# End of attention in a post-norm attention and mixture-of-experts kernel: routing of sequence five at double pace, scatters of sequence six around the last scale, second biases summed ahead of the expert blocks

## The chip, the cores and the metric

The kernel runs on one core of a Trainium2 chip. The metric is the device time of one execution in microseconds. Times of single instructions come from one profiled execution, counted from the start of its span.

## What is computed

Eight sequences of 512 tokens with 128 features go through one layer of causal attention (16 heads of 8) and one layer of experts (14 experts, each token goes to its two best), each with a residual and a normalisation after it:

```python
x = layernorm(x + attention(x))              # Q, K, V, softmax, output projection, biases
probs = softmax(x @ gate_w.T)
top2_p, top2_i = top_k(probs, 2)
w = top2_p / maximum(top2_p.sum(-1), 1e-10)
hh = gelu(einsum('nd,edf->nef', x, w1) + b1)
all_out = einsum('nef,efd->ned', hh, w2) + b2
moe = w[:, 0:1] * all_out[n, top2_i[:, 0]] + w[:, 1:2] * all_out[n, top2_i[:, 1]]
x = layernorm(x + clip(x + moe, -100, 100))
```

The expert outputs are added up with weights, and so are the second biases: for a token this part is the sum of its two weights times the `b2` rows of its two experts. The kernel computes it apart from the experts, as one small matrix product of the weights laid out by expert (`w_all`) with `b2`.

## The kernel before

**Three stages.** Attention first, for all sequences; then the expert blocks; then the sums and the last normalisation. Tokens lie on the 128 partitions, four tiles (`NQ`) to a sequence. Sequences are numbered from zero, so six is the last but one and seven the last.

**Attention runs in steps.** There are 32 units (eight sequences, four groups of four heads) of five steps each. In step `s` the kernel emits the front of step `s` (scores and row maxima), the back of step `s - 12` (scores again, shifted by the maximum, then exponentials on ScalarE and causal selects on GpSimd), and after them whatever has been entered for that step in the table `jobs`. Fronts end at step 159, the last back is at step 171. Each engine takes its instructions in the order in which they are emitted, so a place in `jobs` is a place in the queues of all engines. No planner reorders anything. Jobs of one step run in the order in which they were entered; a job that enters itself again for the next step therefore comes after those that were there from the beginning.

**Jobs around the end.** `product` multiplies the exponentials with the values five and six steps after the back of its unit began, `evacuate` copies the result, `divide`, `project` and `residual` (for the last sequence; others go by way of DRAM with `divisors`, `invert`, `multiply`) give attention plus residual in `y_sb` and its statistics on VectorE. Two steps after `residual`, `route(b)` starts. It is a generator: `proceed` runs it up to its next `yield` once a step, or twice a step for sequence six, its pace. Its pieces are: scale and shift of the normalisation on GpSimd (`layernorm_scale`), normalising on ScalarE, transposes and logits on TensorE, the two best experts on VectorE, a count of the tokens before each one on TensorE, target rows `to_i` on VectorE, two GpSimd operations that fill `w_all`, and then eight indirect DMAs issued from GpSimd, the scatters, one to a piece, which put the token rows into `XS`, sorted by expert.

**The drain.** After the last step `fill` pads the experts' regions in `XS` by DMAs from SP and ScalarE, and VectorE works out which expert each block of 256 rows belongs to. The first block's load waits for all of these writes.

**Expert blocks.** There are 45. `load` brings rows and weights, `turn` transposes (two TensorE transposes and a copy on VectorE), `expert_in` multiplies with the first weights and applies GELU on ScalarE, `expert_out` multiplies with the second weights, scales by the routing weight on VectorE (`ob`) and scatters two tiles to `OS` from GpSimd. `load` runs four blocks ahead, `turn` two, `expert_in` one. After every fourth `expert_out` (blocks 2, 6, 10 and so on) `biases(c)` treats one sequence: a TensorE transpose of `w_all`, a copy on VectorE, a product with `b2_blk` on TensorE, and an addition on VectorE of that product and `y_sb` into a buffer `acc` of its own:

```python
            if i >= 0:
                expert_out(i)
                if i % 4 == 2 and i // 4 < B:
                    biases(i // 4)
```

**The end.** `gather` reads `OS` back, `add_up` sums `acc` and the two gathered parts on TensorE, `residual_2` and `store` clip, add, normalise and write. The result is collected in `z_sb`, which is the region of the input `x_sb`.

## Time and profile before

| | us |
|---|---|
| Median of three runs (643.71 to 650.58) | 649.47 |
| The profiled execution, its own time | 656.64 |
| Its span | 654.9 |
| Last front's maximum begins | 391.34 |
| Copy of the last attention product (`oT`) | 417.57 |
| Last statistics of sequence seven end | 426.45 |
| Rows of the first expert block are loaded from | 456.63 |
| First and last scatter of the expert blocks | 469.02 and 611.63 |

| Engine | busy us | share of the span |
|---|---|---|
| TensorE matmuls | 506.3 | 77% |
| TensorE weight loads (beside the matmuls) | 305.2 | 47% |
| VectorE | 378.4 | 58% |
| GpSimd | 334.6 | 51% |
| ScalarE | 281.7 | 43% |

In rows of groups, of a tile or of an order in time, an instruction stands with its line (L503), its engine (PE is TensorE, PEld its weight loads, DVE VectorE, ACT ScalarE, POOL GpSimd, SP the engine that only issues DMAs), and its output and inputs by the program's names. Groups end with busy time and mean duration in ns, and then the idle time ahead of them and who ended it. Rows in order of time begin with the start and the duration in us. Rows of stretches have the length, then the busy time of PE, PEld, DVE, ACT and POOL with counts, the granted TensorE clock, the DMA share and GB/s. The forty digits of a busy row are tenths of 16.4 us slices.

### The profile page before, as it was taken

To read this page: it belongs to the slowest core of one execution; us is meant where nothing else is said; L and a number is where in the kernel's file an instruction comes from. 1 tells how busy PE (TensorE), PEld (TensorE's weight loads), DVE (VectorE), ACT (ScalarE), POOL (GpSimd) and SP (SyncE) were. 2 spreads that over 40 slices of the span, in tenths; PEclk is the share of its full clock that TensorE was granted. 3 is DMA by queue.
4 is the path that set the end of the run, shared out by engine and by line. 5 is a ranking of instruction groups with operands and counts; after the bars stand their busy time and mean duration, and the time that the engine had idled before them with its cause. 6 is when DMAs were issued, how large, how long until landed. Compare 5 with 4: busy or idle time off the path is not lost.

```text
span 654.9 us, 11179 instructions
## 1 busy us (share of the span) xinstructions
PE 506.3 (77%) x3458; PEld 305.2 (47%) x3458; DVE 378.4 (58%) x835; ACT 281.7 (43%) x437; POOL 334.6 (51%) x690
## 2 busy tenths in 40 slices
PE   2388989899889899799889898620788778777392
PEld 1145545445445455355355354310567667666140
DVE  4267677868848758758668674423344434443185
ACT  0213666666566566466466567210222222232034
POOL 5002333435664664664565767854255646566343
PEclk9865999989879879879699799655788988899696
DMA  5243434444354354253253020114664645553382
GB/s 157 73 146 99 115 99 155 134 139 141 109 163 133 103 162 141 98 173 124 67 162 120 34 71 27 45 44 156 176 170 141 165 138 155 144 152 107 99 206 82
DMA packets 79894, 80.63 MB, mean 123 GB/s; under 512 B 15820, under 2 KB 62005, under 8 KB 79834
## 3 DMA queue, kind: packets, MB, share of 16 engines
q1 hardware_dynamic: 68272, 67.89, 35.5%
q0 software_dynamic: 4928, 8.48, 3.9%
q10 hardware_dynamic: 6634, 3.55, 2.1%
q8 instruction: 27, 0.44, 0.3%
q14 instruction: 33, 0.27, 0.1%
HBM read 51.01 MB, written 31.66 MB: 126 GB/s over the span
## 4 chain that ended last, share of the span: by engine, by line
PE 54%; DVE 14%; ACT 9%; issue 8%; DMA 6%; SPq 4%; POOL 3%; ACTq 1%; another core or an unknown queue 1%; DVEq 0%; POOLq 0%
PE av L503 12%; PE f L360 10%; PE b L446 7%; PE h L940 6%; PE o L956 6%; ACT pt L481 5%; PE f L370 4%; DVE bn L196 2%; DVE mx L400 2%; PE bp L983 2%; DVE stats L197 2%; PE x L926 2%; ACT oT L513 2%; DVE mx L412 1%; DVE ob L964 1%
## 5 line engine op out<-in xcount | busy, mean ns | idle before, releaser
L481 ACT ACTIVATE pt<-b 128x1024 f32<-128x1024 f32 x160 | 162.4, 1023 | 49.6 <-PE b L446 44.7
L457 POOL TENSOR_SCALAR_AFFINE_SELECT pt<-pt 128x256 f32<-128x256 f32 (+1 forms) x224 | 96.2, 444 | 133.6 <-ACT pt L481 132.3
L360 PE MATMUL f<-kr,qr 72*128 72x384 bf16 (+3 forms) x512 | 123.8, 326 | 33.9 <-ACT pt L481 18.3
L220 POOL DMA_INDIRECT OS<-ob,bto_i x90 | 87.6, 974 | 74.1 <-DVE ob L964 36.6
L412 DVE TENSOR_REDUCE mx<-f 128x2 f32<-128x1024 f32 x64 | 78.2, 1224 | 60.5 <-PE f L370 43.7
L446 PE MATMUL b<-qr,kr 75*128 75x384 bf16 (+3 forms) x512 | 102.5, 315 | 6.8 <-DVE mx L400 4.5
L503 PE MATMUL av<-pt,v_aug 128*32 128x512 f32 (+3 forms) x1024 | 96.6, 495 | 3.5 <-POOL pt L457 3.5
L370 PE MATMUL f<-causal_bf,ident_bf 128*128 128x256 bf16 (+1 forms) x320 | 87.1, 272 | 0.0
L360 PEld LDWEIGHTS <-qr 72*128 72x128 bf16 x512 | 53.4, 105 | 71.1 <-issue 49.7
L405 DVE TENSOR_REDUCE mx<-f 128x8 f32<-128x1024 f32 x64 | 77.7, 1222 | 12.8 <-PE f L370 10.9
L945 ACT ACTIVATE hT<-h,wt 128x256 f32<-128x256 f32 x90 | 37.5, 471 | 103.9 <-issue 101.2
L964 DVE TENSOR_SCALAR ob<-o,bxb 128x128 f32<-128x128 f32 x90 | 27.3, 346 | 67.5 <-PE o L956 28.4
L446 PEld LDWEIGHTS <-kr 75*128 75x128 bf16 x512 | 42.8, 101 | 38.6 <-issue 25.7
L956 PE MATMUL o<-wt,hT 128*128 128x128 f32 x360 | 52.9, 293 | 6.2 <-ACT hT L945 2.9
L940 PE MATMUL h<-bxT,wt 128*128 128x256 f32 x180 | 53.7, 427 | 4.9 <-DVE bxT L928 4.7
L503 PEld LDWEIGHTS av<-pt,v_aug 128*32 128x32 f32 x1024 | 29.2, 118 | 59.9 <-issue 43.4
L956 PEld LDWEIGHTS o<-wt,hT 128*128 128x128 f32 x360 | 51.6, 207 | 11.8 <-ACT hT L945 6.6
L400 DVE TENSOR_REDUCE mx<-f 128x4 f32<-128x1024 f32 x32 | 39.1, 1222 | 16.6 <-PE f L370 10.2
L370 PEld LDWEIGHTS <-ident_bf 128*128 128x128 bf16 x320 | 33.8, 106 | 18.9 <-issue 7.8
L220 POOL DMA_INDIRECT XS<-y_sb,to_i x32 | 32.5, 1015 | 13.4 <-issue 7.1
L940 PEld LDWEIGHTS h<-bxT,wt 128*128 128x128 f32 x180 | 34.6, 214 | 9.8 <-DVE bxT L928 5.6
L220 POOL DMA_INDIRECT XS<-second,to_i x32 | 32.2, 1007 | 8.2 <-issue 8.2
(170 smaller groups left out, 583.3 us busy)
## 6 DMA issues: line engine op xcount, KB each, us to landing
wt<-WP SPq DMA_DIRECT2D x45, 257.0 KB
kr<-ksc SPq DMA_DIRECT2D x32, 288.0 KB
qr<-qsc SPq DMA_DIRECT2D x96, 96.0 KB
osc<-oT SPq DMA_DIRECT2D x28, 256.0 KB
bxb<-XS SPq DMA_DIRECT2D x45, 130.0 KB
WP<-in_L_ffn_w_dram SPq DMA_DIRECT2D x28, 128.0 KB
qsc<-qpc SPq DMA_DIRECT2D x24, 128.0 KB
ksc<-kpc SPq DMA_DIRECT2D x24, 128.0 KB
```

Source lines behind the costliest of these rows:

```text
L220: inst = nc.gpsimd.indirect_dma_start(dst, bass.IndirectOffsetOnAxis(ap=idx, axis=0), src, None, bounds_check=bound, oob_is_err=False,)
L360: nc.tensor.matmul(ps[:, col : col + W], qr[u % RING][0:KR, j, qb * P : (qb + 1) * P], kr[u % RING][0:KR, j, :W], start=first, stop=False, ...
L370: nc.tensor.matmul(out, ident_bf, causal_bf[:, 0:n, :], start=False, stop=True, skip_group_check=True,)
L400: nc.vector.reduce_max(mx[:, :, 5], ps.rearrange("p b (s k) -> p (b s) k", s=2), axis=AX.X)
L405: nc.vector.reduce_max(mx[:, j : j + 2, 1:5], ps.rearrange("p b (s k) -> p b s k", k=P), axis=AX.X,)
L412: nc.vector.reduce_max(mx[:, j : j + 2, 7], ps, axis=AX.X)
L446: nc.tensor.matmul(ps[:, col : col + W], kr[u % RING][:, j, kb * P : (kb + 1) * P], qr[u % RING][:, j, kb * P :], start=first, stop=True, ...
L457: nc.gpsimd.affine_select(out=view, in_=view, pattern=[[0, k] for k in n] + [[1, P]], compare_op=ALU.is_ge, fill=0.0, base=0, channel_mult ...
L481: nc.scalar.activation(pt, ps, AF.Exp, scale=SCALE)
L503: nc.tensor.matmul(avs[u][HS * j : HS * (j + 1), kb * P :], v_aug[b % 2][:, kb, g * GH + j, :], p, start=(kb == 0), stop=(kb == 2),)
L940: nc.tensor.matmul(hp[:, f, :], wt[:, f * P : (f + 1) * P], xT, start=True, stop=True)
L956: nc.tensor.matmul(op[:, s, :], hT[:, f, s * P : (s + 1) * P], wt[:, F + f * D : F + (f + 1) * D], start=(f == 0), stop=(f == NFC - 1),)
```

## The change

Five things are changed.

- `biases` moves from the expert stage to the attention stage. It takes its PSUM tile from the caller (in attention one of the three `unit` tiles that backs use), its copy of the weights goes into the buffer of `recT`, and its result into `acc`, which is now the region of `x_sb`. Sequences zero to six are entered as jobs 4, 6, 8, 10, 11, 18 and 20 steps after the last front (step 159); sequence seven stays in the expert stage, at block 2.
- `route(5)` runs at two pieces a step, as `route(6)` did already.
- In the routing of sequence seven, two of the four normalisings go to VectorE.
- `w_all` is filled by a function `weigh`, called after the last scatter, and for sequence six after the first one; for sequence six two more empty pieces stand ahead of the scatters.
- In the expert stage the transposes `x` take a whole PSUM bank each, the biases have one buffer of two banks, and the last sums take the buffers of `x`.

```diff
+    acc = x_sb
+    weighed = set()
+    def biases(c, ps, pool):
+        assert c in weighed
+        ts = slice(c * NQ, (c + 1) * NQ)
+        nc.tensor.transpose(
+            ps[:, 0, 0:P],
+            w_all[:, ts, :].rearrange("p t s -> p (t s)"),
+            ident,
+        )
+        wT = pool.tile([P, T], FP, tag="recT", name=f"wT_{c}", bufs=1)[:, 0:P]
+        nc.vector.tensor_copy(wT, ps[:, 0, 0:P])
+        nc.tensor.matmul(
+            ps[:, 1, :], wT, b2_blk.rearrange("p t d -> p (t d)"), start=True, stop=True
+        )
+        nc.vector.tensor_tensor(
+            acc[:, ts, :],
+            ps[:, 1, :].rearrange("p (t d) -> p t d", d=D),
+            y_sb[:, ts, 0:D],
+            ALU.add,
+        )
...
                 t = b * NQ + i
+                if b == B - 1 and i % 2 == 1:
+                    nc.vector.tensor_scalar(
+                        y_sb[:, t, 0:D],
+                        y_sb[:, t, 0:D],
+                        rstd[:, i : i + 1],
+                        shift[:, i : i + 1],
+                        ALU.mult,
+                        ALU.add,
+                    )
+                    continue
                 nc.scalar.activation(
...
-            wide = rt("wide", [2, NQ, E])
-            nc.gpsimd.tensor_tensor(
-                wide, hot, w.unsqueeze(3).to_broadcast([P, 2, NQ, E]), ALU.mult
-            )
-            nc.gpsimd.tensor_tensor(w_all[:, ts, 0:E], wide[:, 0], wide[:, 1], ALU.add)
-            yield
+            def weigh():
+                weighed.add(b)
+                wide = rt("wide", [2, NQ, E])
+                nc.gpsimd.tensor_tensor(
+                    wide, hot, w.unsqueeze(3).to_broadcast([P, 2, NQ, E]), ALU.mult
+                )
+                nc.gpsimd.tensor_tensor(
+                    w_all[:, ts, 0:E], wide[:, 0], wide[:, 1], ALU.add
+                )
+            for _ in range(3 if b == B - 2 else 1):
+                yield
             for i in range(NQ):
                 for k, src in enumerate((y_sb[:, b * NQ + i, :], second[:, i, :])):
                     scatter("XS", XS[:, :], to_i[:, k, i : i + 1], src, E * CAP - 1)
+                    if b == B - 2 and i == 0 and k == 0:
+                        weigh()
                     yield
+            if b != B - 2:
+                weigh()
...
-                at(r + 2, proceed, r + 2, route(b), 2 if b == B - 2 else 1)
+                at(r + 2, proceed, r + 2, route(b), 2 if b in (B - 3, B - 2) else 1)
+        last_front = step_of(NU - 1, UN - 1)
+        for c, n in enumerate((4, 6, 8, 10, 11, 18, 20)):
+            at(last_front + n, lambda c: biases(c, unit(f"b2_{c}"), work), c)
...
-        name="ps_b", bufs=2, space=bass.MemoryType.PSUM
+        name="ps_b", bufs=1, space=bass.MemoryType.PSUM
...
-            tp = ps_x.tile([P, BT], FP, tag="x", name=f"x_{i}")
+            tp = ps_x.tile([P, T], FP, tag="x", name=f"x_{i}")[:, 0:BT]
...
-                if i % 4 == 2 and i // 4 < B:
-                    biases(i // 4)
+                if i == 2:
+                    biases(B - 1, ps_b.tile([P, 2, T], FP, tag="b2", name="b2_ps", bufs=1), ffn)
...
-            sums[c] = ps_b.tile([P, NQ, D], FP, tag="b", name=f"sum_{c}")
+            sums[c] = ps_x.tile([P, NQ, D], FP, tag="x", name=f"sum_{c}")
```

More of the change, by code (lines that the diff above doesn't have):

```diff
@@ L967, in expert_out @@
                 scatter("OS", OS[:, :], to_i[:, s : s + 1], ob[:, s, :], 2 * N - 1)
-        acc = ffn.tile([P, NT, D], FP, tag="acc", name="acc", bufs=1)
-        def biases(c):
-            ts = slice(c * NQ, (c + 1) * NQ)
-            wp = ps_b.tile([P, T], FP, tag="b", name=f"wp_{c}")
-            nc.tensor.transpose(
-                wp[:, 0:P],
-                w_all[:, ts, :].rearrange("p t s -> p (t s)"),
-                ident,
-            )
-            wT = ffn.tile([P, P], FP, tag="wT", name=f"wT_{c}")
-            nc.vector.tensor_copy(wT, wp[:, 0:P])
-            bp = ps_b.tile([P, T], FP, tag="b", name=f"bp_{c}")
-            nc.tensor.matmul(
-                bp, wT, b2_blk.rearrange("p t d -> p (t d)"), start=True, stop=True
-            )
-            nc.vector.tensor_tensor(
-                acc[:, ts, :],
-                bp.rearrange("p (t d) -> p t d", d=D),
-                y_sb[:, ts, 0:D],
-                ALU.add,
-            )
         AHEAD = 4
```

## The prediction, made before the result was known

> **What bounds the kernel now.** I read the page first, then tables by stretch, the chain in order of time, and the order of single instructions at the two places that the change touches. The profiled execution took 656.64 us, 654.9 of them span; the median of the runs shown is 649.47, so sums made in the trace are carried over to the median as differences.
>
> ```profile
> PE   2388989899889899799889898620788778777392
> PEclk9865999989879879879699799655788988899696
> L220 POOL DMA_INDIRECT OS<-ob,bto_i x90 | 87.6, 974 | 74.1 <-DVE ob L964 36.6
> L503 PE MATMUL av<-pt,v_aug 128*32 128x512 f32 (+3 forms) x1024 | 96.6, 495 | 3.5 <-POOL pt L457 3.5
> ```
>
> The busy rows show three stages: attention bound by TensorE up to about 400 us, a hole around 410 to 459 us (the drain: last backs, routing of the last two sequences, block plan), and the expert blocks to about 612 us. The change moves work from the third stage into the second, so both are to be priced. The stretches, with TensorE's busy time first and its granted clock near the end:
>
> ```profile
> 391.34:412.90 21.56, 18.50 (x154) 8.92 (x152) 10.37 (x36) 15.48 (x22) 16.97 (x39) 1.00 0.13 40
> 412.90:458.94 46.04, 12.84 (x60) 7.62 (x60) 15.68 (x72) 3.82 (x9) 28.02 (x45) 0.50 0.26 81
> 479.62:572.45 92.83, 73.77 (x414) 62.39 (x414) 39.18 (x155) 23.30 (x56) 54.53 (x57) 0.91 0.55 153
> 578.83:606.52 27.69, 19.52 (x122) 16.61 (x122) 10.70 (x46) 7.60 (x19) 17.52 (x18) 1.00 0.42 117
> ```
>
> 391.34 is where the last front ends. For 21.6 us after it TensorE is still 86% busy; the hole opens only later. In the drain the set of waits that counts is this one, GpSimd's:
>
> ```profile
> 425.77 0.97 POOL L220 DMA_INDIRECT XS<-y_sb,to_i  x1 [0.31 <-issue]
> 426.27 0.18 DVE L197 BATCH_NORM_AGGREGATE stats<-bn 128x2 f32<-128x6 f32 x1
> 427.04 0.98 POOL L220 DMA_INDIRECT XS<-second,to_i  x1 [0.30 <-issue]
> 428.33 0.97 POOL L220 DMA_INDIRECT XS<-y_sb,to_i  x1 [0.30 <-issue]
> 429.37 0.20 POOL L204 TENSOR_SCALAR rstd<-stats 128x4 f32<-128x4 f32 x1
> 431.30 1.65 ACT L645 ACTIVATE y_sb<-y_sb,shift,rstd 128x128 f32<-128x128 f32 x4 [9.50 <-POOL shift L207]
> ```
>
> The last statistics are there at 426.45, the scale starts at 429.37: 2.9 us behind sequence six's scatters. In the expert stage the biases and the scatters:
>
> ```profile
> L983 PE MATMUL bp<-b_blk,wT x16: 592/697/1061, 474.2 to 569.2; 128*128 128x512 f32 x16
> L986 DVE TENSOR_TENSOR acc<-bp,y_sb x8: 691/691/692, 476.1 to 569.8; 128x512 f32<-128x512 f32 x8
> PE bp L983 <- DVE wT L981: 13.8, 6, 3.3
> ...
> 578.83 0.97 POOL L220 DMA_INDIRECT OS<-ob,bto_i  x1 [1.57 <-DVE ob L964]
> ...
> 588.08 0.97 POOL L220 DMA_INDIRECT OS<-ob,bto_i  x1 [1.89 <-DVE ob L964]
> ...
> 597.32 0.97 POOL L220 DMA_INDIRECT OS<-ob,bto_i  x1 [1.87 <-DVE ob L964]
> ...
> 606.52 0.97 POOL L220 DMA_INDIRECT OS<-ob,bto_i  x1 [1.84 <-DVE ob L964]
> ```
>
> TensorE stands still at six of the eight biases, 13.8 us in all, for a copy that VectorE makes late. But the last four rows come after the last bias: even without biases GpSimd issues six scatters 1.28 us apart (three blocks), waits 1.9 us, and so on, 9.24 us a turn.
>
> **What the Trainium skill says.** "TensorE: Matmul & The Clock Gate", section "What's actually happening": the array falls to half clock after an idle window of about 3.4 us and needs as long a busy one to come back. The trace agrees: clock 1.00 until 412.9, then 0.50, and a bias matmul takes 592 to 1061 ns. "Perfetto Trace Analysis", section "Tensor Engine Instruction": a matmul's end is estimated, and the other engines' queues are strict FIFO. Both are seen here: the eviction of block 13 starts at 511.62 though its matmuls are drawn as over at 509.2, and ScalarE's normalising of sequence six stood behind the scale. So I count by starts of evictions and scatters, not by drawn matmuls.
>
> **The change part by part.**
>
> *Seven biases leave the expert blocks* (the one at the third block stays). Two readings. By scatters: blocks 3 to 31 span 479.62 to 572.45, 92.83 us for 28 blocks, 3.31 a block; the bias-free turns give 27.69 us for 9 blocks, 3.08. 28 x 0.238 = 6.7 us. By TensorE: the output matmuls of blocks 31 and 43 start at 570.73 and 603.87, 2.76 a block, and 28 x 0.55 = 15.5 us. The stage ends with the last scatter, at 612.6, so I stay near the first and take **8.5 us gained**; ends 3 (the middle bias cycle of four blocks, 12.72 us, against 12.31, seven times) and 15.5. Late next: GpSimd's scatters, 2.56 us a block at least.
>
> *Five biases (sequences zero to four) in the last back steps, 163 to 170.* Each is a transpose (0.27), a round trip to VectorE (copy 0.28, handed on in some 0.1 each way) and two matmuls at full clock (0.86 start to start): 1.6 us of TensorE, in order, 8.0 in all. The second stands behind residual of sequence six on VectorE: in the trace of before that row of work runs 399.05 to 401.93 while TensorE would be at the bias from about 400.2, so 1.8 us more of standing still, with backs, exponentials and the products of sequence seven queued behind. Against it: TensorE has 4.6 us of gaps between 391.34 and 417.5 (4.1 of them waits on selects that stand behind sequence five's scatters, or on ScalarE), which the biases fill, and the products at 414.6 run at half clock, 1.5 us more than before 412.9. Sum: 8.0 + 1.8 - 4.1 - 1.5 = +4.2 us at the last evacuation (417.57 now). The evictions with y (0.69 each) lie on VectorE, 52% idle there.
>
> *Sequence five at double pace.* It takes eight scatters (10.2 us of GpSimd) out of 403 to 418.8, where selects waited on them; that gain is in the 4.1 above. They now come two a step in steps 155 to 159: 10.2 + seven selects x 0.44 + maximum pieces 0.9 = 14.2 us on GpSimd in five steps of 2.1 us = 10.5. It falls 3.7 us behind; a product follows its selects by two steps (4.2 us), so it is nearly hidden. Its copy to `second` enters SP's queue at step 149, seven steps ahead of the scatter that reads it: nothing. VectorE's wait for the weights' reciprocal now falls into a step with a front. Cost taken +1, ends 0 and 4 (cover gone, and the clock with it).
>
> *Sequence six's scatters around the last scale.* From the last evacuation to the last statistics it is 8.88 us now; with a clock still full for transposes and projection I take 8.0: statistics at 417.57 + 5.2 + 8.0 = 430.8 against 426.45. Three scatters and the two weighing operations (0.37 and 0.34) stand ahead of the scale instead of five and two; begun at about 423 to 424.5 they are done by then. The 2.9 us queue goes; the scale starts at 430.8 against 429.37, **+1.4**. The five scatters behind it need 6.4 us and the next GpSimd work of routing comes some 9 us later: nothing.
>
> *Half of the last normalising on VectorE.* ScalarE's four take 1.65; two would save 0.8. But the biases of sequences five and six are ahead in VectorE's queue, each waiting for TensorE: copy 0.28, matmuls 1.1 (1.9 at half clock), eviction 0.69, twice, then two normalisings of 0.28: the last is ready 4.9 to 6.7 us after the statistics, where it is 3.6 us after the scale's start now. Net **+1.6**, ends 0.5 and 2.8.
>
> *Weighing after the scatters* for sequence seven: the first scatter some 0.7 us sooner. The first block's load waits for the fill's copies (landed 456.06), not for scatters (about 454.4): nothing. The *x* region as accumulator and the changed PSUM pools add no wait that I see: nothing.
>
> Drain: **+3.0 us**, ends -3 and +8. Sum 3.0 - 8.5 = -5.5: profiled 651.1, median **644.0**.
>
> **Rivals.** (1) *The expert stage is TensorE's*: the standing still (13.8 us) and the half clock behind it go in full, 15.5, and the drain is even: 634.0. For it: the waits on the copy; against: the bias-free turns. (2) *Scatters set the stage*: only 3 us gained and the drain 3.5 worse: 650.0. For it: GpSimd never leaves its 1.28 us beat but for 1.9 us. (3) *Slower: attention's end becomes TensorE's round trips.* Place: the five biases in steps 163 to 170. If each, not one, finds VectorE occupied for 1.8 us, that is 5 x 3.4 = 17.0 - 5.6 = +11.4, the gaps put the clock to half early, and the drain ends 10 us later with 3 gained: 656.5. It decides once the last evacuation comes later than about 427. Against it: VectorE has idle time of 2 to 5 us in front of several of its operations there.
>
> **Numbers.** Likeliest 0.45 (its own range 639 to 649), (1) 0.25, (2) 0.18, (3) 0.12. About half of the likeliest's chance lies below 643.0, which is 1% under the median and about what a measurement tells from no change. Faster 0.25 + 0.20 = 0.45; within 1% 0.25 + 0.18 = 0.43; slower 0.12. The range leaves out the far half of (1) and most of (3): 633 to 652.
>
> **What would show it.** Right: scatter turns of three blocks from the fourth block on, 126 us from the scatter of block 3 to that of block 44 (132.0 now); last evacuation at 421 to 424; no scatter between the last statistics and the scale; VectorE's normalising after the seventh bias's eviction. Wrong: turns of two blocks still (then another stall made them), a last evacuation before 418, or a first block's load later than 463.

## The result

The changed kernel takes 657.8 us (median of 16 runs, 647.8 to 663.0), the kernel before beside it 649.3 (16 runs, 643.4 to 652.6). The ratio is 1.0146, 95% interval 1.0098 to 1.0194: slower by 1.5%. The forecast was 644.0 with a range of 633 to 652. Here and below ratios, and the medians of the fourth four, leave disturbed runs out; other medians are of all runs.

The profiled execution of the changed kernel took 655.18 us, its span 653.5. That is 1.5 us less than the one of before, though the medians stand the other way: single executions of one kernel differ by several us, much of it ahead of the changed code. The maxima of step 120, which the change does not touch, came at 302.3 us before and at 296.0 after. So I count from the start of the reduction of maxima of step 144 (358.09 before, 351.33 after).

| us after step 144 | before | after |
|---|---|---|
| last evacuation (copy of the last `oT`) | 59.5 | 72.6 |
| first block's load | 98.5 | 110.1 |
| first block's load to last scatter | 156.3 | 150.9 |
| last scatter to the end | 42.0 | 41.2 |

The end of attention is 13 us longer, where the forecast had 5.2. The expert blocks are 5 us shorter in this one trace; two later traces of the same kernel (154.6 and 155.7) do not repeat that. (The last scatter of before begins at 612.91; the 611.63 of the table ahead is the one in front of it.)

The 13 us split at the start of the exponential of step 163 on ScalarE; in that step the first of the moved sums is issued. First the kernel before, from step 144 to there and from there to the last evacuation, then the changed kernel:

```profile
358.09:396.32 38.23, 35.64 (x290) 18.56 (x293) 27.14 (x47) 23.12 (x33) 25.85 (x60) 0.91 0.18 59
396.32:417.57 21.25, 16.59 (x137) 7.60 (x129) 7.62 (x31) 11.73 (x18) 17.22 (x33) 0.89 0.10 33
351.33:397.74 46.41, 37.43 (x287) 18.55 (x290) 27.80 (x53) 23.43 (x32) 36.37 (x75) 0.87 0.19 60
397.74:423.93 26.19, 21.79 (x151) 10.44 (x147) 10.02 (x31) 12.21 (x17) 7.51 (x19) 0.90 0.04 11
```

So 8.2 us are lost ahead of the sums, and 4.9 where they are.

The profile page of the kernel after, TensorE's busy row, its clock and two groups (columns as before):

```profile
PE   2388989899799898898998877861577678867392
PEclk9865999999879899699699987965598998798797
L245 POOL DMA_INDIRECT OS<-ob,bto_i x90 | 87.5, 972 | 67.8 <-DVE ob L1015 32.2
L528 PE MATMUL av<-pt,v_aug 128*32 128x512 f32 (+3 forms) x1024 | 93.1, 485 | 2.1 <-POOL pt L482 2.1
```

The scatters still take 0.97 us each, and the idle time of GpSimd ahead of them is still 67.8 us (74.1 before). The stretches, the first from the last front to the last evacuation:

```profile
389.12:423.93 34.81, 27.88 (x176) 12.25 (x175) 12.29 (x35) 15.67 (x22) 14.98 (x34) 0.80 0.06 17
423.93:463.77 39.84, 12.14 (x46) 6.57 (x46) 17.33 (x77) 3.04 (x7) 22.83 (x38) 0.58 0.28 88
482.98:571.22 88.24, 67.50 (x398) 58.87 (x397) 34.54 (x143) 23.61 (x57) 54.41 (x57) 0.92 0.56 155
```

34.8 us, where it was 26.2 (391.34 to 417.57), and the clock is 0.80 of full speed, where it was 1.00 for the first 21.6 of them. Around the last scale, in order of time:

```profile
430.80 0.18 DVE L197 BATCH_NORM_AGGREGATE stats<-bn 128x2 f32<-128x6 f32 x1
431.31 1.01 POOL L245 DMA_INDIRECT XS<-second,to_i  x1 [0.49 <-issue]
432.62 0.97 POOL L245 DMA_INDIRECT XS<-y_sb,to_i  x1 [0.30 <-issue]
433.67 0.20 POOL L204 TENSOR_SCALAR rstd<-stats 128x4 f32<-128x4 f32 x1
435.59 0.88 ACT L680 ACTIVATE y_sb<-y_sb,shift,rstd 128x128 f32<-128x128 f32 x2 [8.35 <-POOL shift L207]
436.52 0.69 DVE L228 TENSOR_TENSOR x_sb<-b,y_sb 128x512 f32<-128x512 f32 x1 [2.24 <-ACT y_sb L680]
437.13 0.61 DVE L671 TENSOR_SCALAR y_sb<-y_sb,rstd,shift 128x128 f32<-128x128 f32 x2
```

Two scatters still stand between the last statistics (430.98) and the scale (433.67): the queue of 2.9 us became one of 2.7. VectorE's normalising stands behind the seventh sum, as forecast. In the expert blocks, four scatters ahead of which GpSimd stood for over 1 us:

```profile
581.34 0.97 POOL L245 DMA_INDIRECT OS<-ob,bto_i  x1 [1.55 <-DVE ob L1015]
...
590.63 0.97 POOL L245 DMA_INDIRECT OS<-ob,bto_i  x1 [1.92 <-DVE ob L1015]
...
596.95 0.97 POOL L245 DMA_INDIRECT OS<-ob,bto_i  x1 [1.51 <-DVE ob L1015]
...
603.37 0.97 POOL L245 DMA_INDIRECT OS<-ob,bto_i  x1 [1.38 <-DVE ob L1015]
```

The stops of 1.4 to 1.9 us are there without the sums. From the first scatter of block 3 to the last of block 44, which is the count of all that follows, it is 129.3 us, where it was 133.3. From first scatter to first scatter, as the forecast counted, it is 128.1 where it was 132.0, and the forecast said 126.

### The profile page after: what moved, and what is told of

Read it like the earlier page. It is cut to its first block, busy times and chain, and to the rows that moved or that the text cites. A ratio compares the mean times of both kernels' runs of the same rounds, so it can differ in the third digit from the quotient of the medians.

```text
span 653.5 us, 11189 instructions
## 1 busy us (share of the span) xinstructions
PE 500.8 (77%) x3458; PEld 301.1 (46%) x3458; DVE 378.1 (58%) x837; ACT 281.2 (43%) x435; POOL 334.6 (51%) x690
## 4 chain that ended last, share of the span: by engine, by line
PE 44%; DVE 14%; issue 11%; DMA 10%; ACT 8%; SPq 8%; POOL 4%; ACTq 1%; DVEq 0%; POOLq 0%
PE av L528 11%; PE f L385 8%; PE b L471 6%; ACT pt L506 4%; DMA bxb<-XS 4%; PE h L991 3%; PE f L395 3%; PE o L1007 3%; DVE bn L196 2%; DVE stats L197 2%; PE x L977 2%; DVE mx L425 2%; PE b L225 2%; DMA qr<-mt 2%; POOL XS L245 1%
## 5 line engine op out<-in xcount | busy, mean ns | idle before, releaser
L385 PE MATMUL f<-kr,qr 72*128 72x384 bf16 (+3 forms) x512 | 121.5, 321 | 33.7 <-ACT pt L506 15.7
L245 POOL DMA_INDIRECT OS<-ob,bto_i x90 | 87.5, 972 | 67.8 <-DVE ob L1015 32.2
L528 PE MATMUL av<-pt,v_aug 128*32 128x512 f32 (+3 forms) x1024 | 93.1, 485 | 2.1 <-POOL pt L482 2.1
L430 DVE TENSOR_REDUCE mx<-f 128x8 f32<-128x1024 f32 x64 | 77.7, 1222 | 10.5 <-PE f L395 8.3
L977 PE MATMUL x<-ident,bxb 128*128 128x128 f32 x90 | 19.9, 306 | 35.3 <-DMA bxb<-XS 32.4
```

The source lines that it names most:

```text
L245: inst = nc.gpsimd.indirect_dma_start(dst, bass.IndirectOffsetOnAxis(ap=idx, axis=0), src, None, bounds_check=bound, oob_is_err=False,)
L385: nc.tensor.matmul(ps[:, col : col + W], qr[u % RING][0:KR, j, qb * P : (qb + 1) * P], kr[u % RING][0:KR, j, :W], start=first, stop=False, ...
L430: nc.vector.reduce_max(mx[:, j : j + 2, 1:5], ps.rearrange("p b (s k) -> p b s k", k=P), axis=AX.X,)
L528: nc.tensor.matmul(avs[u][HS * j : HS * (j + 1), kb * P :], v_aug[b % 2][:, kb, g * GH + j, :], p, start=(kb == 0), stop=(kb == 2),)
```

## The experiments

The theory after the result (theory A) had the loss in two places, the pairs of scatters in steps 155 to 160 and the round trips of the five sums on TensorE, with 5 to 7 us gained in the expert blocks. The rivals were that either of the two places is the whole loss, and that the blocks give more or nothing. From the second four on the blocks were taken to give nothing, and the question was how pace and sums work together, and whether the sums cost TensorE's waits for VectorE's copies or its own time. The runs were made on five occasions, on chips of different speed: the kernel before took 611.7, 653.2, 614.1, 654.0 and 610.5 us on them. Times of whole kernels are compared within an occasion only. Steps of attention are about as long on all of them, and their lengths are compared throughout; two traces of one kernel still differ there by up to 1.7 us (f_sums and changed_pace_one below, 61.3 and 63.0 from step 144 to the last evacuation).

Steps are told apart by the start of their exponential on ScalarE. "TensorE's idle time" is the length of a stretch less its busy time.

### First four: which part loses

**pace_alone**: the kernel before, sequence five at double pace.

```diff
-                at(r + 2, proceed, r + 2, route(b), 2 if b == B - 2 else 1)
+                at(r + 2, proceed, r + 2, route(b), 2 if b in (B - 3, B - 2) else 1)
```

> Only sequence five's double pace, put into the kernel before. Theory A (the loss has two seats: the pair of scatters per step ahead of the selects in steps 155 to 160, 4.5 us, and the biases' round trips on TensorE, 8.6 us): last front 4 to 5 us later than before, the last evacuation within 2 us of before's since sequence five's scatters are gone from there, total within 3 us of before. Rival B (double pace is harmless, what the changed kernel lost ahead of step 160 was a stall by chance): last front within 1 us, total 4 to 6 us faster than before. Rival C (double pace is the whole loss): 5 us slower or more.

Measured 614.62 against 611.74, ratio 1.0011 (0.9963 to 1.0059). The trace has the exponentials of steps 162 and 163 8.8 us apart (2.2 in the kernel before), and the last evacuation at 63.5 us after step 144, 4 us later than before, where theory A had at most 2.

**biases_alone**: the change with pace, weighing and normalising as before, so that only the sums are moved.

```diff
-                at(r + 2, proceed, r + 2, route(b), 2 if b in (B - 3, B - 2) else 1)
+                at(r + 2, proceed, r + 2, route(b), 2 if b == B - 2 else 1)
-                if b == B - 1 and i % 2 == 1:
+                if False:
-            for _ in range(3 if b == B - 2 else 1):
-                yield
+            weigh()
+            yield
```

> Only the seven biases moved into the attention stage, with the accumulator in the region of x and the PSUM pools of the change; pace, weighing, yields and normalising as before. Theory A: last front as before, last evacuation 8 to 12 us later, expert stage (first load to last scatter) 5 to 6 us shorter, total 3 to 8 us slower than before. Rival C (double pace is the whole loss): total 3 us faster or more. Rival D (the expert stage is TensorE's, prediction's first rival): expert stage 12 to 16 us shorter.

Measured 616.76, ratio 1.0141 (1.0087 to 1.0194), of only six executions; the profiled one was the shortest of them (613.04) and shows no loss up to the first load (98.4 us after step 144). Its ratio does not fit two runs below of a kernel that differs from it in the weighing and the normalising alone (0.9993 and 0.9994). That stays open, and with it whether the sums by themselves lose nothing: one of three runs says otherwise.

**no_seven**: the kernel before without the sums of sequences zero to six, which are left out of the output.

```diff
-                if i % 4 == 2 and i // 4 < B:
-                    biases(i // 4)
+                if i == 2:
+                    biases(B - 1)
```

> The kernel before with the second biases of sequences zero to six left out (the sums take y itself in the place of y plus bias); sequence seven's stays at block 2. It measures what seven biases cost in the expert stage, with nothing put into the drain. Theory A: expert stage 5 to 7 us shorter, total 5 to 7 us faster than before. Rival D: 12 to 16 us faster. Rival E (scatters alone set the stage): 0 to 3 us.

Measured 613.76, ratio 1.0031 (0.9995 to 1.0067). Block 3 to block 44 took 105.96 us, and 105.94 to 105.95 in the two kernels of this occasion that had the sums there (pace_alone) or all ahead of the blocks (late); in biases_alone it was 107.0. **Seven sums less in the expert blocks are worth nothing here**, where theory A had 5 to 7 us. This is one of the chips with the shorter times; the run was not made on one with the longer times, such as the one that the forecast is about.

**late**: the kernel before with all eight sums behind the block plan.

```diff
+        for c in range(9):
+            if c < 8:
+                ps = unit(f"b2_{c}")
+                units[c] = ps, bias_weights(c, ps, work)
+            if c >= 1:
+                bias_sum(c - 1, *units.pop(c - 1))
```

> The kernel before with all eight biases behind the block plan, where TensorE and VectorE stand idle until the first block's rows land (449.8 to 458.9 in the kernel before); the transposes run one sequence ahead of the sums. Theory A: the drain gets 0 to 3 us longer since the last sums end after the rows have landed, the expert stage starts at full clock and gets 6 to 10 us shorter, total 4 to 9 us faster than before. Rival E: total within 2 us of before.

Measured 612.75, ratio 1.0033 (1.0001 to 1.0064): no gain, where theory A had 4 to 9 us, and if anything a loss of 0.3%. That is as in no_seven, which does not have the seven sums at all, so put here they cost nothing that shows. Why no gain, this timeline of GpSimd shows:

```profile
499.83 0.97 POOL L246 DMA_INDIRECT OS<-ob,bto_i  x1 [0.30 <-issue]
501.11 0.98 POOL L246 DMA_INDIRECT OS<-ob,bto_i  x1 [0.30 <-DVE ob L999]
502.40 0.97 POOL L246 DMA_INDIRECT OS<-ob,bto_i  x1 [0.30 <-issue]
```

A scatter every 1.28 us, two to a block, without a pause from block 3 to block 44: 41 steps from block to block of 2.55 us.

### Second four: the change itself, with one thing less

**changed** is the change itself.

> The changed kernel itself once more, beside the kernel before and the three below. In the last four kernels the expert stage kept the scatters' beat of 1.28 us with biases (105.95 us from block 3 to the end of the stage) and without (105.96). Theory A2 (biases cost nothing in the expert stage, so taking them out gains nothing; double pace and biases together lengthen attention's end): last evacuation 8 to 13 us later after step 144 than the 60.6 us of the kernel without seven biases, expert stage within 1 us, total 6 to 11 us slower than before. Rival F (the long end of attention in the first trace of the changed kernel was one bad execution): 60 to 64 us to the last evacuation and total within 4 us.

Measured 661.9 against 653.24, ratio 1.0179 (1.0121 to 1.0237), of six executions. Last evacuation 72.7 us after step 144, the first load 111.6 us; block 3 to block 44 133.4 us, so that the 4 us which the first trace showed there are gone.

**changed_late**: the change with its seven sums behind the block plan.

```diff
-        for c, n in enumerate((4, 6, 8, 10, 11, 18, 20)):
-            at(last_front + n, lambda c: biases(c, unit(f"b2_{c}"), work), c)
```

> The changed kernel with its seven biases taken out of the back steps and put behind the block plan, all else of the change kept. Theory A2: attention's end as with double pace alone, 62 to 65 us to the last evacuation after step 144, then 3 to 4 us less to the first block's load since the scale waits for two scatters less and the first scatter for no weighing: total within 3 us of before, and 5 to 9 us faster than the changed kernel. Rival C2 (double pace, the scatters' new place and the normalising on VectorE are the loss): 5 us slower than before or more.

Measured 651.29, ratio 0.9997 (0.9962 to 1.0032); last evacuation at 61.8, first load at 98.8. **With the sums out of the last steps the whole loss is gone.** Up to step 157 the two traces run alike within 0.1 us.

**mixed_pace**: the kernel before, sequence five at double pace up to its row numbers, then one scatter a step.

```diff
-            for _ in range(pace):
+            for _ in range(pace if step < slow else 1):
```

> The kernel before with sequence five routed at double pace only as far as its target rows, and its eight scatters one a step (steps 155 to 163). Theory A2 (the pairs of scatters, not the earlier routing, hold up the selects): no stall of over 4 us in steps 158 to 164, last evacuation 2 to 5 us earlier than the kernel before, total 1 to 5 us faster. Rival G (the time lost to scatters moves with them, whatever the spacing): last evacuation within 1.5 us of before, total within 2 us.

Measured 654.56, ratio 1.0002 (0.9968 to 1.0035). Its trace has the last evacuation at 56.8 us after step 144, 2.7 us sooner than that of before, which the time does not show.

**changed_no_trip**: the change, with the identity in the place of the copied weights in the five products, so that those sums are not computed.

```diff
-            ps[:, 1, :], wT, b2_blk.rearrange("p t d -> p (t d)"), start=True, stop=True
+            ps[:, 1, :], ident if c < 5 else wT, b2_blk.rearrange("p t d -> p (t d)"), start=True, stop=True
```

> The changed kernel with the five biases of the back steps multiplied by the identity, in the place of the weights that VectorE has just copied: transposes, copies, matmuls and additions stay, and TensorE no longer waits for the copy (so those five sums are not the reference's). Theory A2, round trips as the cost: 4 to 8 us faster than the changed kernel, last evacuation earlier by as much. Rival H (TensorE's own time for the biases is the cost, not the wait): within 2 us of the changed kernel.

Measured 664.47, ratio 1.0185 (1.0120 to 1.0249). It tells nothing about the waits, because they are still there: 5.2 us on TensorE's weight loads for the copy, as in the changed kernel. The likely reason is that product and turned weights share a PSUM tile, so that the product still waits for the copy out of that tile; no run separates that.

### Third four: the waits, the pace, and what holds the expert blocks

**ahead**: a job turns the weights of the next sequence and then multiplies those that the job before turned and copied.

```diff
+        def ahead(c):
+            ps = unit(f"b2_{c}")
+            if c < 4:
+                turn_weights(c + 1, ps)
+            nc.tensor.matmul(ps[:, 1, :], held.pop(c), ...)
+            if c < 4:
+                copy_weights(c + 1, ps)
```

> The changed kernel with the five sums of the last steps of attention taken one job ahead: a job turns the weights of the next sequence and then multiplies those that the job before had turned and copied, so that TensorE has no copy to wait for (in the earlier kernel with the identity in the place of the copied weights the wait was still there: TensorE's idle time in steps 163 to 171 was 4.3 us, as in the changed kernel). Theory (TensorE is full in these steps, and the five sums add their own 6.9 us of it and 3.9 us of waiting for the copies): the exponentials of steps 163 to 171, 23.4 us apart in the changed kernel and 13.0 without the five, come to 19 to 20, TensorE's idle time there to under 1.5 us, and the ratio to the kernel before to 1.010 to 1.014. Rival (the waits for VectorE are the loss, as the prediction's slower case had it): 14 to 16.5 us, and a ratio of 1.002 to 1.006.

Measured 618.33 against 614.14, ratio 1.0109 (1.0077 to 1.0140). TensorE's idle time in steps 163 to 171 fell from 4.3 us to 0.16 and the stretch from 23.4 to 16.45 us, which is the rival's number; the last evacuation came at 65.9 us, not at 72.7:

```profile
392.51:408.96 16.45, 16.29 (x114) 8.33 (x110) 7.18 (x22) 11.04 (x15) 6.13 (x16) 0.92 0.06 18
```

The waits, with what follows from them, are about two thirds of what the sums cost in these steps of the trace (6.9 of 10.4 us, with changed_late's 13.0 for the stretch without sums). My theory, which had most of it as TensorE's own time, was wrong in the trace, though the ratio lies in the range that I gave for it: in the time less comes back, since this kernel is still 1.1% slower than the one before, where changed_late is not slower.

**changed_pace_one**: the change with sequence five at single pace (the diff of pace_alone undone).

> The changed kernel with sequence five routed at single pace, all else as in the change. Theory (the double pace is no part of the loss in time, as the kernel with nothing but the double pace said): a ratio to the kernel before of 1.014 to 1.019, as the changed kernel; the exponentials of steps 162 and 163 are 2 to 3 us apart where the changed kernel had 4.5 to 6.6, those of 163 to 171 still 21 to 24. Rival (the double pace and the sums make each other worse): 1.004 to 1.011, with 163 to 171 under 19.

Measured 614.22, ratio 0.9993 (0.9962 to 1.0025), below both expectations. Yet steps 163 to 171 take 24.1 us, as in the change; the 10 us that it is ahead at the last evacuation (63.0 against 72.7) lie ahead of step 163. So neither the pace alone (pace_alone) nor the sums alone lose in this time: the question of the fourth occasion.

**late_mixed**: changed_late and mixed_pace together.

> The changed kernel with its seven sums behind the block plan and sequence five at double pace only as far as its row numbers, its scatters one to a step. If the gains that the two traces showed add up (last evacuation at 56.8 in place of 59.5 to 60.6 us after step 144, and 21.0 in place of 23.5 from there to the block plan), the first load comes 92 to 95 us after step 144 where the kernel before has 98.5, and the ratio is 0.990 to 0.995. Rival (the differences of a few us between single traces are not of the kernel, since either kernel alone gave no gain in time): 0.997 to 1.002.

Measured 610.60, ratio 0.9961 (0.9931 to 0.9991); first load at 96.5. Both lie between the two expectations: less than the sum of the two gains, more than nothing. The last evacuation came at 60.2 us, so mixed_pace's 56.8 is not found again.

**one_scatter**: the kernel before without the second scatter of each block, which is left out; the rows are filled with x at the start.

```diff
-                scatter("OS", OS[:, :], to_i[:, s : s + 1], ob[:, s, :], 2 * N - 1)
+                if s == 0:
+                    scatter("OS", OS[:, :], to_i[:, s : s + 1], ob[:, s, :], 2 * N - 1)
```

> The kernel before with the second scatter of each expert block left out, 45 in the place of 90; the rows of results are filled with x at the start so that the last stage has something to read. Theory (GpSimd's scatters set the pace of the expert stage, which is why sums taken out of it gained nothing): the time from the scatter of block 3 to that of block 44, 106 us on the chip with the shorter times and 131 to 133 on the other, falls to 92 to 98 or to 92 to 108, where TensorE's own 2.2 us a block sets it. Rival (TensorE sets it, as the prediction's first rival had it): within 3 us of the kernel before.

The kernel was executed once. Block 3 to block 44 took 96.4 us, in the range of the theory (what held it there, the last two runs tell). With the scatters thinned out, VectorE's queue (scaled results and sums, in order of time) shows what a sum costs:

```profile
504.95 0.61 DVE L966 TENSOR_SCALAR ob<-o,bxb 128x128 f32<-128x128 f32 x2 [0.76 <-PE o L958]
506.97 0.69 DVE L989 TENSOR_TENSOR acc<-bp,y_sb 128x512 f32<-128x512 f32 x1 [1.22 <-PE bp L986]
508.95 0.61 DVE L966 TENSOR_SCALAR ob<-o,bxb 128x128 f32<-128x128 f32 x2 [0.68 <-PE o L958]
510.92 0.61 DVE L966 TENSOR_SCALAR ob<-o,bxb 128x128 f32<-128x128 f32 x2 [0.76 <-PE o L958]
```

A block follows the one before after 1.97 us, but after 4.00 us with a sum between them. Seven such sums are 14 us, near the 15.5 us of TensorE that the prediction's first rival counted, and where all scatters are issued none of it shows (no_seven).

### Fourth four: pace and sums, each alone, both and neither

All four have the other edits of the change. f_both is the change, f_sums has single pace (the kernel of changed_pace_one), f_pace has the seven sums behind the plan (the kernel of changed_late), f_neither has both of these.

> The changed kernel again, for the comparison of four on one chip: the five sums in the last back steps and sequence five at double pace. Either theory: a ratio to the kernel before of 1.012 to 1.018, the last evacuation 72 to 76 us after step 144 begins, exponentials of steps 163 to 171 about 23 us apart.

> The five sums in the last back steps, sequence five at single pace, all else as in the change. Shared slack (GpSimd's selects hold the end of attention back by 4 us while sequence five's scatters are mixed with them, and that covers the sums): last evacuation 60 to 64 us after step 144, 3.0 us after the last exponential; ratio 0.998 to 1.004. Adding up (the sums lose by themselves): 1.006 to 1.013, last evacuation 65 or later.

> Sequence five at double pace, the seven sums behind the block plan, all else as in the change. Shared slack: last evacuation 61 to 64 us after step 144, 2.7 us after the last exponential, 8 us between the exponentials of steps 162 and 163; ratio 0.996 to 1.002. Adding up with the loss on the side of the pace: over 1.004.

> The seven sums behind the block plan and sequence five at single pace, all else as in the change. Either theory: last evacuation 59 to 61 us after step 144, 6.6 to 7.0 us after the last exponential, 1.6 to 2.2 us between the exponentials of steps 162 and 163; ratio 0.993 to 1.001. Shared slack: the differences of the two single edits to this kernel sum to under half of that of both together; adding up: to that of both within 3 us.

The kernel before took 652.8 us.

| | f_neither | f_pace | f_sums | f_both |
|---|---|---|---|---|
| median us | 648.4 | 651.1 | 652.3 | 664.0 |
| ratio | 0.9943 | 0.9954 | 0.9994 | 1.0160 |
| its interval | 0.9915 to 0.9971 | 0.9929 to 0.9980 | 0.9948 to 1.0039 | 1.0104 to 1.0217 |
| step 144 to last evacuation | 57.3 | 62.4 | 61.3 | 72.9 |
| exponentials of steps 163 to 171 | 15.1 | 13.4 | 20.8 | 23.3 |
| TensorE idle in these | 2.3 | 0.5 | 5.0 | 4.3 |
| last exponential to last evacuation | 6.4 | 2.7 | 4.2 | 3.1 |

The pace adds 2.7 us to the median, the sums 3.9, both 15.6: the two singles make two fifths of both, where shared slack was to give under half. In the traces it is 5.2 and 4.0 against 15.6. **Together the two lose more than each by itself.** The ratio of one kernel moves by 0.4% from occasion to occasion (changed_late 0.9997, f_pace 0.9954), so the single effects are hardly clear of noise; the 15.6 are. The stretches from the exponential of step 144 to that of 163, and from 163 to 171, first of f_neither:

```profile
352.02:388.27 36.25, 32.69 (x286) 18.07 (x288) 26.33 (x47) 23.43 (x33) 25.23 (x61) 1.00 0.20 62
388.27:403.36 15.09, 12.82 (x104) 6.68 (x96) 4.70 (x20) 11.02 (x17) 10.90 (x22) 0.93 0.09 28
```

of f_pace:

```profile
354.22:401.09 46.87, 36.37 (x291) 18.43 (x293) 27.91 (x53) 23.90 (x33) 36.30 (x76) 0.92 0.18 59
401.09:414.45 13.36, 12.88 (x103) 6.70 (x99) 3.23 (x13) 10.85 (x15) 6.02 (x16) 0.90 0.07 20
```

of f_sums:

```profile
385.88:406.65 20.77, 15.73 (x116) 8.21 (x108) 8.67 (x29) 11.06 (x17) 13.79 (x28) 1.00 0.10 30
```

and of f_both:

```profile
351.07:398.11 47.04, 36.32 (x291) 18.39 (x293) 27.89 (x53) 23.82 (x33) 36.37 (x76) 0.91 0.19 59
398.11:421.36 23.25, 18.91 (x115) 8.81 (x111) 7.70 (x23) 11.18 (x16) 6.85 (x18) 0.88 0.04 13
```

The pace puts 11.1 us more of GpSimd's work (36.30 against 25.23) ahead of step 163 and makes that stretch 10.6 us longer. It gets 1.7 us back up to step 171 and 3.7 us behind it, because selects no longer stand behind sequence five's scatters. After that TensorE is busy for 12.88 of 13.36 us: there is next to no idle time left for sums to fill. At single pace GpSimd holds the end back by itself (6.4 us from the last exponential to the last evacuation), and sums that delay the exponentials get 2.2 us of their 5.7 back there. They do not fill TensorE's idle time, which rises from 2.3 to 5.0 us. But the clock is at half for part of f_neither's stretch (0.93) and full in f_sums (1.00), while with the pace it goes from 0.90 to 0.88: the sums add 2.9 us to TensorE's busy time at single pace and 6.0 at double. Of the 6.4 us that both lose beyond the two singles, 2.6 lie behind the last exponential and 3.1 in this busy time; that the clock is the reason for the 3.1 is argued, not shown. How the pace stops TensorE, in f_pace's order of time:

```profile
396.58 1.01 POOL L269 DMA_INDIRECT XS<-second,to_i  x1 [0.51 <-issue]
397.62 0.39 POOL L805 TENSOR_TENSOR wide<-hot,w 128x112 f32<-128x112 f32 x1
398.08 0.30 POOL L808 TENSOR_TENSOR w_all<-wide 128x56 f32<-128x56 f32 x1
398.34 1.71 POOL L506 TENSOR_SCALAR_AFFINE_SELECT pt<-pt 128x256 f32<-128x256 f32 x4
399.15 0.64 PE L552 MATMUL av<-pt,v_aug 128*32 128x128 f32 x4 [3.63 <-POOL pt L506]
```

Four selects stand behind the last scatter and the weighing; TensorE waits 3.63 us for the first of them. And the waits that the sums bring, from f_both's table of waits in steps 163 to 171 (engine, line and what it waited for, then us in total, times, and the longest):

```profile
DVE wT L224 <- PE b L218: 12.1, 3, 9.1
ACT pt L506 <- PE b L471: 9.9, 5, 3.9
PEld b L225 <- DVE wT L224: 5.2, 5, 2.4
```

Five times TensorE stands at a product for the copy, and ScalarE's exponentials behind it wait 9.9 us for scores.

f_neither beats the kernel before (by 0.6%, on this one occasion) and, by 15.6 us, the changed one. It is the change with single pace for sequence five, and with the seven sums out of the last steps.

### Last two

**one_scatter_no_seven**: one_scatter and no_seven together, which leaves out the second scatters and seven sums.

> The kernel before with the second scatter of each expert block left out (the rows of results filled with x at the start) and with the second biases of sequences zero to six left out. Theory (GpSimd's beat hides what the sums cost TensorE): the scatter of block 44 comes 41 x 1.98 = 81 to 84 us after that of block 3 on a chip with the shorter times, where it was 96 to 97 with the sums and 106 with all scatters; so taking the sums out gains 13 to 15 us here and nothing where all scatters are issued. On the chip with the longer times also under 90, since the stalls there come only with dense scatters. Rival (something other than the sums and the scatters holds the blocks): 92 us or more.

The kernel was executed once. Block 3 to block 44 took 96.7 us: the rival's case. My theory, that without scatters the sums' 14 us would show as gain, was wrong. SP's issues say what comes next:

```profile
500.28 0.38 SPq L915 DMA_DIRECT2D bxb<-XS  x1
500.92 0.33 SPq L921 DMA_DIRECT2D wt<-WP  x1
502.65 0.38 SPq L915 DMA_DIRECT2D bxb<-XS  x1
503.29 0.33 SPq L921 DMA_DIRECT2D wt<-WP  x1
505.13 0.38 SPq L915 DMA_DIRECT2D bxb<-XS  x1
```

SP issues the two loads of a block and, in the 1.4 us between, reads the two addresses into registers, almost without a pause: 2.37 to 2.48 us a block in these rows. TensorE waited for the rows, 10.7 us in 18 waits over 85 us; in one_scatter it was 1.2 us in one. So three things lie close together: scatters at 2.55 us a block, SP's loads at 2.4, TensorE at 1.97 plus 2.03 for a sum in every fourth, some 2.5 on average. Taking work out of one that does not set the pace gains nothing. That SP's loads hold the blocks once both others are thinned out is read from this one trace; no run shortens them.

**ahead_one**: ahead with sequence five at single pace.

> The changed kernel with the five sums' weights turned one job ahead, so that TensorE has no copy to wait for, and with sequence five at single pace. If slack of GpSimd's selects covers TensorE's own 5.5 to 6.5 us for the five sums: last evacuation 57 to 60 us after step 144, as with no sums there (57.3), TensorE idle under 1.5 us in steps 163 to 171, ratio 0.993 to 0.999. If TensorE's own time is what costs at single pace too: last evacuation 61 or later, as with the waits (61.3), ratio 0.999 to 1.005.

Measured 610.10 against 610.51, ratio 0.9960 (0.9921 to 0.9998). Last evacuation 58.1 us after step 144, TensorE idle for 0.4 us in steps 163 to 171, which take 15.9 us. Without the waits and with GpSimd's slack still there the five sums cost about 1 us (57.3 in f_neither), less than two traces of one kernel differ. Slack covers TensorE's own time, the first of the two cases.

## Why the prediction was wrong

The forecast had 3.0 us more up to the first block's load and 8.5 less behind it. The load came 11.6 us later (98.5 to 110.1 after step 144), and the blocks gave next to nothing back. Two of its terms failed, the price of the double pace and the gain in the blocks; the term of the five sums came out by luck.

**Sequence five at double pace, +1 us, ends 0 and 4.** This step failed by most. Ahead of step 163 the change loses 8.2 us against the kernel before, and f_pace 10.6 against f_neither, which differ in the pace alone. The queue of 3.7 us on GpSimd was seen. That a product follows its selects by two steps did not hide it, because the product that waits (3.63 us above) stands in TensorE's own queue, ahead of the backs behind it. Most of it is idle time of TensorE, 6.4 of the 8.2 us (9.0 against 2.6) and 6.9 of the 10.6 (10.5 against 3.6). The rest is more busy time for almost the same instructions, in f_pace at a granted clock of 0.92 where f_neither has 1.00. What the pace gives back behind step 163 is 5.5 us (from there to the last evacuation 16.0 in f_pace, 21.5 in f_neither); this is the gain that the forecast had as the 4.1 us of gaps in the sum below. Net the pace costs 5.2 us in these traces, where +1 and −4.1 make a gain.

**Five sums in steps 163 to 170, +4.2 us.** From the exponential of step 163 to the last evacuation it is 21.3 us before and 26.2 after, +4.9, so the sum was near; its parts were not, and the errors cancel. In the prediction's terms, at double pace: own time and round trips, 8.0, are 3.5 us where the waits are gone (19.5 in ahead, 16.0 in f_pace). The one wait of 1.8 us is 6.8 (26.3 in f_both, 19.5 in ahead), since TensorE stood at each of the five products, 4.2 us in all, and with what followed. The gain of 1.5 by a full clock did not come: it was 0.89 from step 163 to the last evacuation before and 0.90 after. The −4.1 for gaps is the 5.5 us that the pace gave. So 3.5 + 6.8 − 5.5 = 4.8 us. One gain was taken for two edits, as the prediction said itself, and put into the sum once; but it belongs to the pace, and without the pace the sums did not fill those gaps (idle 5.0 us in f_sums, 2.3 in f_neither).

**Seven sums out of the expert blocks, −8.5 us.** Failed. With all eight sums the traces of the slower chips have 133.3 us from block 3 to block 44 (before, mixed_pace), with one left 129.3 to 133.4, mean 131.7 of eight: 1.6 us, less than the eight differ among themselves. On the chip of no_seven it was nothing. The reading by scatters took the difference between turns with and without a sum for the price of the sum; turns of two and of three blocks are there without sums as well. It did not ask what SP's queue does. Rival 2 (3 us) was the nearest.

**Last evacuation to statistics, 8.0 us.** 7.1 in the trace after, 8.0 in f_both: right. So is the whole from the last evacuation to the first load, 1.5 us less than before where the forecast's terms make 2.2 less. **The 2.9 us queue at the scale goes.** It did not: 2.7 after, 1.8 in f_both. Sequence six's scatters were to begin at 423 to 424.5; like everything that is tied to steps they moved with the drain. **Half of the normalising on VectorE, +1.6.** Right in kind: from the scale's start to the last normalising it was 3.6 us before, 4.1 after and 5.0 in f_both, but 2.8 in f_neither and f_pace, where no sums stand ahead. The edit was a gain that another edit of the change took away.

**The slower rival** named the place, TensorE's round trips in steps 163 to 170, and 656.5 us, 1.3 from what was measured. Its mechanism is two thirds of what the sums cost in these steps, by ahead. The number is near by luck: it had 11.4 us there, where the change lost 4.9 against before, and next to nothing ahead of step 163, where it lost 8.2. Only one of the five products found VectorE occupied for about 2 us; the others waited 0.4 to 0.8. Its point of decision, an evacuation later than 427 us, misled: 423.9 was read, because that execution was 6.8 us early at step 144. On the clock of before it would be 430.7.

## What to carry to other kernels

Work that is moved to an earlier place in an engine's queue delays what stands behind it there. A lag of some steps is no cover if the instruction that then waits stands in the queue of the fullest engine: it holds up that engine's whole queue. Before booking work into an engine's gaps, ask what makes the gaps, and whether another edit of the same change removes it; then price the edits alone and together. Work that crosses engines inside a full stretch should be split so that its first half is issued one turn ahead: behind step 163 the same five sums cost 3.5 us that way, where they had cost 10.3. Where one engine sets the pace of a stage, find the next two before pricing work on the others.

## What the runs showed of the hardware

The clock falls to half without a long standstill. In f_neither it is at half from 401.3 us on, and TensorE's longest idle time in the 10 us before was 1.1 us; in f_both it is at half from 407.1, after one of 2.25 us. In the kernel before it fell at 412.95, with no idle time of TensorE over 1.02 us in the 10 us ahead of it, so that this fall, for which the prediction said that the trace agrees with the rule of one idle window, does not show that rule. The Trainium skill, "TensorE: Matmul & The Clock Gate", section "A second HAM failure mode: psum-queue depth-cycling", tells of half clock after frequent short pauses, and these traces agree with it: in the 6.8 us before the fall in f_neither TensorE was busy for 4.9. The rule of one idle window of 3.4 us, on which the prediction rested, is too kind here. No threshold can be read from these runs: in f_sums the clock stayed full past an idle time of 2.97 us at 390.7.

Chips differ in the expert blocks: 106 to 109 us from block 3 to block 44 on those with the shorter times and 129 to 133 on the others, with the same program. On the slower ones SP's loads lie 3.2 us apart on average (140.7 us from the first to the last of 45 in f_neither) and GpSimd waits for results. Which of the two comes first, no run here settles: those with fewer scatters ran on chips with the shorter times.
